# Four graph layers in one kernel: the rows of layer 2's next block are made two to three chunks sooner, and layer 1 gets one more step before its row of scores

## The chip, the cores and the metric

The kernel runs on one core of a Trainium2 chip. A core has a matrix engine (TensorE, PE in the profile, with its weight loads as PEld), a vector engine (VectorE, DVE), an activation engine (ScalarE, ACT), a general engine (GpSimd, POOL) and an engine that here only issues transfers (SyncE, SP). The metric is device time in microseconds; the figure of a kernel is the median of its runs.

## The reference

The input is a matrix x of 2708 nodes by 512 features, and an adjacency matrix adj of 2708 x 2708 with ones on its diagonal. Four layers follow each other. Each adds a graph operation to x and normalises the rows:

```python
x = layernorm(x + L0(x, adj))   # attention with 8 heads, masked by adj
x = layernorm(x + L1(x, adj))   # D^-1/2 (adj+I) D^-1/2 ((x W1' + b1) W2' + b2)
x = layernorm(x + L2(x, adj))   # additive attention, below
x = layernorm(x + L3(x, adj))   # relu(D^-1/2 (adj+I) D^-1/2 x W)
```

The change is in layers 1 and 2. Layer 2 is

```python
s1 = (h @ W[:512]) @ a_w ;  s2 = (h @ W[512:]) @ a_w
e = s1[:, None] + s2[None, :] + a_b
e = where(e >= 0, e, 0.2 * e) ;  e = where(adj > 0, e, -9e15)
out = softmax(e, axis=1) @ (h @ fc_w + fc_b)
```

So a score needs one number of the query node (s1) and one of the key node (s2). The softmax needs, for each query, the largest score, and because the leaky step only rises, that is found from the largest s2 among the query's neighbours.

## The kernel before

The 2708 nodes are 22 chunks of 128 rows, the last of 20. They are also 6 blocks (NB) of 512 columns, the last of 148, which is 4 chunks a block and 2 in the last. All data is fp32.

**Layer 1** (graph1 L828, finish1 L857). For each block b of output columns graph1 goes over the 22 chunks m: it loads a piece of the transposed adjacency (adjT, load_adjT L607, on SP's queue, eight buffers), multiplies it with H[m] into two PSUM banks, and adds up column sums on DVE (L848). The rest of block b is done by finish1(b), a generator that is advanced while the *next* block is being multiplied, once after every chunk m with m % 4 == 3: at each step one chunk is mapped, added and normalised, and its score s2 is computed as a **column** (score L703, L707: one number per partition, in s2c). When all chunks of the block are through, one further step turns the columns into a **row** that is the same on all 128 partitions (spread_block L645, spread L635: for every chunk one matmul of the broadcast column with the identity, two PE instructions each, into a PSUM tile psds, then one ACT copy L643 into s2b). What is left of the generator is run off after the block, before the next generator is made. Block 5's finish1 is advanced in the first part of layer 2, after every odd chunk.

The row s2b is read by top2 (L696, L698): for 128 query rows it takes the largest of s2 over their neighbours in a stretch of adj. For block 0 this is done during layer 1 in three pieces (piece L898, top0 L908), the second piece of each of its four chunks at chunks 0 to 3 of block 5; that piece ends at column 2048, so it reads the rows of blocks 0 to 3. Its loads have two buffers, and they stand in SP's queue among the adjT loads.

**Layer 2** (graph2 L1007, weigh L787, softmax2 L773, product L726). For a block b of 512 queries and each chunk m of 128 keys, ACT masks the adjT piece (L694) and makes the leaky scores from the query row s1b and the key column s2c (Prelu, L781), DVE subtracts the mask (L782) and the row of maxima mxb (L783), ACT takes Exp (L784), PE multiplies the result pt with x into four PSUM banks (L731, 8 PE instructions a chunk), and POOL adds up the sums (L795). There are six pt buffers, eight adjT buffers, six accumulator banks and two further PSUM banks (ps_m) for everything else.

Block 0 is done in two parts: chunks 0 to 15 with preliminary maxima while the last nodes are still being normalised, and chunks 16 to 21 afterwards with the final ones.

The two rows that a block needs, s1b and mxb, come from row_lines (L770): again columns into rows by spread, 8 PE instructions and one ACT copy each. The columns for block b + 1 come from class Maxima (L936), whose steps are taken while block b is multiplied: one step begins two loads of adj, each of the other eight masks half a stretch of adj, takes its largest s2, and every second one ends with row_max (L755), which writes a column of mxc. In blocks 1 and later the steps are taken after even chunks, so the ninth comes after chunk 16. For block 1 six of them are taken in the first part of block 0 and three after chunks 16, 17 and 18. The call of row_lines stands in the loop at L1072, after chunk 20.

The finished block is mapped with fc_w by finish2 (L1025), also a generator: ACT copies four accumulators (L1037), and after chunks 3, 7, 11 and 15 of the next block one chunk each is multiplied (L743, tile pf in ps_m), added by DVE (L1048) and normalised.

**What sets the order.** In layer 0 the order on PE, DVE and ACT is written out by hand. From layer 1 on it is made by the framework's planner when the kernel is built: it goes through the instructions by its own estimates of their durations, gives each engine what is ready, earliest in the program first, and fixes one order for each engine. On the chip each engine then keeps to that order. A few instructions (held, for Maxima and its loads) are pinned behind what precedes them in the program on their engine.

Of the kernel before, what the change touches and what calls it, by code (L numbers as in the profile page):

```python
# [22 lines left out]
def kernel(  # L23
# [27 lines left out]
    NC = (N + P - 1) // P  # L51
    NB = (N + BLK - 1) // BLK
    QSCALE = 1.0 / KD**0.5

    def rows(c):
        return c * P, min(P, N - c * P)

    def cols(b):
        return b * BLK, min(BLK, N - b * BLK)

    def chunks_of(b):
        n0, w = cols(b)
        return [n0 // P + i for i in range((w + P - 1) // P)]
# [37 lines left out]
    def layernorm(dst, y, q):  # L101
        st = small.tile([P, 6], F32, tag="lnst", name="lnst")
        nc.vector.bn_stats(st[:q], y)
        mv = small.tile([P, 2], F32, tag="lnmv", name="lnmv")
        nc.vector.bn_aggr(mv[:q], st[:q])
        ve = small.tile([P, 1], F32, tag="lnve", name="lnve")
        nc.vector.tensor_scalar(ve[:q], mv[:q, 1:2], LN_EPS, None, ALU.add)  # L107
        rs = small.tile([P, 1], F32, tag="lnrs", name="lnrs")
        rsqrt(rs[:q], ve[:q], q, 1, "ln")
        nc.vector.tensor_scalar(dst, y, mv[:q, 0:1], rs[:q], ALU.subtract, ALU.mult)  # L110
# [524 lines left out]
    def spread(dst, columns, name):  # L635

        w = sum(q for _, q in columns)
        pd = ps_m.tile([P, BLK], F32, tag="m", name=f"psd{name}")
        o = 0
        for col, q in columns:  # L640
            nc.tensor.matmul(pd[:, o : o + q], col.to_broadcast([q, P]), ident[:q, :q], start=True, stop=True)
            o += q
        nc.scalar.copy(dst, pd[:, :w])  # L643

    def spread_block(dst, cols_of, b, name):  # L645
        spread(dst, [(cols_of[: rows(c)[1], c : c + 1], rows(c)[1]) for c in chunks_of(b)], name)

    def column_sums(sums, b, name):

        w = cols(b)[1]  # L650
        pc = ps_m.tile([P, 4], F32, tag="m", name=f"pcs{name}")
        for i, c in enumerate(chunks_of(b)):
            q = rows(c)[1]
            nc.tensor.matmul(pc[:q, i : i + 1], sums[:, i * P : i * P + q], ones, start=True, stop=True)
        return pc
# [47 lines left out]
    def score(dst, c, of, held=False):  # L703

        q = rows(c)[1]
        pr = io.tile([P, D], F32, tag="y", name=f"pr{of}_{c}")
        tt = nc.vector.tensor_tensor_reduce(  # L707
            out=pr[:q],
            in0=X[c][:q],
            in1=ub[:q, of, :],  # L710
            scale=1.0,
            scalar=0.0,
            op0=ALU.mult,
            op1=ALU.add,
            accum_out=dst[:q, c : c + 1],
        )
        if held:
            tc.keep_in_program_order(tt)
        if of == 0:
            nc.vector.tensor_scalar(dst[:q, c : c + 1], dst[:q, c : c + 1], gab_sb[:q], None, ALU.add)  # L720

    def accs(name):

        return [ps_acc.tile([P, BLK], F32, tag="acc", name=f"acc{name}_{k}") for k in range(KC)]
# [45 lines left out]
    def row_lines(b, maxs, name=""):  # L770
        return row_line(b, s1c, "s1b"), row_line(b, maxs, "mxb")
# [26 lines left out]
    if True:  # L798
# [58 lines left out]
        def finish1(b):  # L857

            n0, w = cols(b)
            yt, sums = done1[b]  # L860
            pc = column_sums(sums, b, f"1_{b}")
            for i, c in enumerate(chunks_of(b)):
                q = rows(c)[1]
                rc = small.tile([P, 1], F32, tag="rc1", name=f"rc1_{c}")
                nc.vector.tensor_tensor(rc[:q], pc[:q, i : i + 1], rdeg[:q, c : c + 1], ALU.mult)
                p2 = ps_m.tile([P, BLK], F32, tag="m", name=f"p2_{c}")
                for hc in range(HC):
                    nc.tensor.matmul(
                        p2[:q, :], yt[:, hc, i * P : i * P + q], w2_sb[:, hc, :], start=(hc == 0), stop=(hc == HC - 1)
                    )  # L870
                y = io.tile([P, D], F32, tag="y", name=f"y1_{c}")
                nc.vector.scalar_tensor_tensor(y[:q], b2_sb[:q], rc[:q], X[c][:q], ALU.mult, ALU.add)
                nc.vector.scalar_tensor_tensor(y[:q], p2[:q, :], rdeg[:q, c : c + 1], y[:q], ALU.mult, ALU.add)
                layernorm(X[c][:q], y[:q], q)
                score(s2c, c, 1)
                yield
            spread_block(s2b[:, n0 : n0 + w], s2c, b, f"s2_{b}")
            yield

# [126 lines left out]
    if True:  # L1006
        def graph2(b):  # L1007
            m0 = CUT // P if b == 0 else 0
            acc = accs(f"2_{b}")
            sums = cap2.tile([P, BLK], F32, tag="cs", name=f"cs2_{b}")  # L1010
            for m in range(m0, NC):
                weigh(b, m, acc, sums, m0)
                yield m
            done2[b] = acc, sums

        def first_part(yt):

            f = io.tile([P, BLK], F32, tag="y", name="f2")
            nc.vector.tensor_tensor(f, lines_a[1], lines[0][1], ALU.subtract)
            nc.scalar.activation(f, f, AF.Exp)  # L1020
            for k in range(KC):
                nc.vector.tensor_tensor(yt[:, k, :], acc_a[k], f, ALU.mult)
            nc.vector.tensor_tensor(sums_a, sums_a, f, ALU.mult)

        def finish2(b):  # L1025
            w = cols(b)[1]
            cs = chunks_of(b)
            acc, sums = done2[b]
            if b == 0:
                yt = yt0  # L1030
                for k in range(KC):
                    nc.vector.tensor_tensor(yt[:, k, :], yt[:, k, :], acc[k], ALU.add)
                nc.vector.tensor_tensor(sums, sums, sums_a, ALU.add)
            else:
                yt = ytp.tile([P, KC, BLK], F32, tag="yt", name=f"yt2_{b}")
                for k in range(KC):
                    nc.scalar.copy(yt[:, k, :w], acc[k][:, :w])  # L1037
            yield
            pc = column_sums(sums, b, f"2_{b}")
            rc = small.tile([P, 4], F32, tag="rc2", name=f"rc2_{b}")  # L1040
            for i, c in enumerate(cs):
                q = rows(c)[1]
                nc.vector.reciprocal(rc[:q, i : i + 1], pc[:q, i : i + 1])
            for i, c in enumerate(cs):
                q = rows(c)[1]
                pz = mapped(yt, i, q, fcw_sb, f"pf{c}")
                y = io.tile([P, D], F32, tag="y", name=f"y2_{c}")
                nc.vector.scalar_tensor_tensor(y[:q], pz[:q, :], rc[:q, i : i + 1], X2[c][:q], ALU.mult, ALU.add)  # L1048
                layernorm(X2[c][:q], y[:q], q)
                yield  # L1050

        def scaled(c):

            q = rows(c)[1]
            nc.vector.tensor_scalar(X[c][:q], X2[c][:q], rdeg[:q, c : c + 1], None, ALU.mult)

        yt0 = ytp.tile([P, KC, BLK], F32, tag="yt", name="yt2_0")
        first_part(yt0)
        fin = iter(())
        for b in range(NB):  # L1060
            if b:
                queue = Maxima(b + 1) if b + 1 < NB else None
            for m in graph2(b):
                if m % 4 == 2 and 0 <= m // 4 < len(chunks_of(b)) and b:
                    c = chunks_of(b)[m // 4]
                    q = rows(c)[1]
                    held(nc.vector.tensor_tensor(X2[c][:q], X[c][:q], fcb_sb[:q], ALU.add))
                if queue and (b == 0 or m % 2 == 0):
                    queue.step()
                if m % 4 == 3:  # L1070
                    next(fin, None)
                if b + 1 < NB and m == NC - 2:  # L1072
                    lines[b + 1] = row_lines(b + 1, mxc)
                if b == NB - 1 and m >= 6:
                    scaled(m - 6)
                if b == 0 and m == NC - 1:
                    for c in chunks_of(0):
                        held(nc.vector.tensor_tensor(X2[c], X[c], fcb_sb, ALU.add))
            for _ in fin:
                pass  # L1080
            fin = finish2(b)
            next(fin)
        for c in range(NC - 6, chunks_of(NB - 1)[0]):
            scaled(c)
# [224 lines left out]
```

## Time and profile before

| | us |
|---|---|
| median of 3 runs (lowest, highest) | 2607.38 (2600.11, 2610.36) |
| the profiled execution | 2611.59 |
| its span, first to last instruction | 2609.8 |
| layer 0 (0 to about 1345 us), PE busy | 1317.5 of 1345 |
| layer 0's end and layer 1 (1345 to 1650), PE busy | 301.1 of 305 |
| first part of layer 2 and its seam (1650 to 1735), PE busy | 74.6 of 85 |
| rest of layer 2 (1735 to 2160), PE busy | 415.3 of 425 |
| layer 3 (2160 to 2610), PE busy | 431.8 of 450 |

How to read it: a row of the waits gives the engine, the line that waited, what released it, the total in us, the number of times, and the longest. A row of the timeline gives start and length in us, the engine, the line, the operation, output and inputs with their shapes, and in brackets how long the engine was idle before it and what ended that. The windows give the busy time of an engine in a stretch with the clock that TensorE was granted (1.00 is full speed). Matmuls in fp32 appear as two PE instructions each.

### The profile page before, as it was taken

Reading aid. Unit: us, or ns where it says so; the run is one execution under the profiler, and the core shown is the slowest. Engines: PE = TensorE matmul, PEld = TensorE weight load, DVE = VectorE, ACT = ScalarE, POOL = GpSimd, SP = SyncE. Lnnn points to the kernel's source line nnn. Section 1 sums busy time; section 2 is a strip of 40 time slices with the busy share of each in tenths; the row PEclk is TensorE's granted clock in tenths of the full one; section 3 lists DMA queues with packets and bytes.
Section 4 is the critical chain, followed back from the end, with each engine's and each line's share of the span. In section 5 each row is a group of like instructions: output and inputs, shape, how many; then the busy total and the mean of one; then the engine's idle time right before and its main releaser. Section 6 shows DMA issues by size and latency. Waiting matters only on the chain.

```text
span 2609.8 us, 42027 instructions
## 1 busy us (share of the span) xinstructions
PE 2540.3 (97%) x15263; PEld 1472.2 (56%) x15263; DVE 1874.5 (72%) x4576; ACT 1212.1 (46%) x2417; POOL 312.0 (12%) x322
## 2 busy tenths in 40 slices
PE   8999999999999999999899999899999999999997
PEld 3445666767676766676546444444444456444465
DVE  2004999999999999998484678978767775453544
ACT  1113778788787787887211001566555640000000
POOL 1110000000000000000220000234333330000000
PEclk9999999999999999999899999989999999999999
DMA  5012888888988888888772544354434213644633
GB/s 199 32 53 58 215 230 217 222 220 209 240 206 210 229 217 216 229 209 184 208 219 76 134 119 139 112 166 135 123 100 129 62 30 108 180 143 141 181 100 107
DMA packets 221445, 411.45 MB, mean 158 GB/s; under 512 B 28711, under 2 KB 48857, under 8 KB 221238
## 3 DMA queue, kind: packets, MB, share of 16 engines
q1 hardware_dynamic: 214998, 392.03, 56.3%
q0 software_dynamic: 6240, 16.73, 1.8%
q8 instruction: 121, 1.98, 0.3%
q14 instruction: 86, 0.70, 0.1%
HBM read 213.57 MB, written 16.72 MB: 88 GB/s over the span
## 4 chain that ended last, share of the span: by engine, by line
PE 77%; issue 9%; DVE 6%; DMA 4%; SPq 2%; ACT 1%; POOL 0%; POOLq 0%; DVEq 0%; ACTq 0%
PE pss L310 15%; PE av L417 14%; PE acc L731 13%; PE acc L837 7%; PE m L1141 6%; PE pf L743 3%; PE psv L250 3%; PE psk L223 3%; PE pst L390 3%; PE psq L223 3%; DMA e<-d 2%; PE po L677 2%; PE ph L823 1%; DVE d L361 1%; SPq L371 1%
## 5 line engine op out<-in xcount | busy, mean ns | idle before, releaser
L332 DVE CUSTOM_DVE_ANT_0 s<-pss,adj 128x512 f32<-128x512 f32 (+1 forms) x1020 | 574.2, 618 | 27.6 <-PE pss L310 26.5
L354 ACT ACTIVATE s<-s,nm 128x1024 f32<-128x1024 f32 (+1 forms) x510 | 527.7, 1037 | 22.9 <-DVE nm L347 22.0
L310 PE MATMUL pss<-KT,qt 64*128 64x512 f32 (+1 forms) x2016 | 463.8, 565 | 7.7 <-DVE mx L332 7.4
L361 DVE STREAM_TRANSPOSE d<-s 128x1024 f32<-128x1024 f32 x340 | 402.4, 1222 | 18.1 <-DMA e<-d 9.0
L731 PE MATMUL acc<-pt,x 128*128 128x512 f32 (+1 forms) x880 | 341.0, 547 | 12.6 <-ACT pt L784 9.7
L417 PEld LDWEIGHTS av<-e,V 128*64 128x64 f32 x5376 | 295.6, 137 | 62.6 <-issue 32.9
L417 PE MATMUL av<-e,V 128*64 128x128 f32 x5376 | 327.4, 275 | 0.0
L310 PEld LDWEIGHTS pss<-KT,qt 64*128 64x128 f32 x2016 | 194.2, 186 | 145.3 <-issue 69.3
L731 PEld LDWEIGHTS acc<-pt,x 128*128 128x128 f32 x880 | 161.1, 196 | 192.1 <-issue 166.0
L837 PE MATMUL acc<-at,h 128*128 128x512 f32 (+1 forms) x504 | 196.8, 543 | 0.0
L795 POOL TENSOR_TENSOR cs<-cs,pt 128x512 f32<-128x512 f32 (+2 forms) x110 | 157.3, 1430 | 202.8 <-ACT pt L784 199.5
L782 DVE TENSOR_TENSOR pt<-pt,at 128x512 f32<-128x512 f32 (+2 forms) x132 | 106.2, 812 | 80.7 <-ACT pt L781 80.5
L1171 ACT ACTIVATE z<-pz,rdeg 128x512 f32<-128x512 f32 (+1 forms) x22 | 15.1, 688 | 312.0 <-PE pz L743 312.0
L438 POOL DMA_DIRECT2D otd<-ot x84 | 45.2, 538 | 959.7 <-ACT ot L437 947.3
L93 ACT ACTIVATE ln_t<-lnve 128x1 f32<-128x1 f32 x88 | 17.7, 201 | 305.7 <-DVE lnve L107 305.7
L391 ACT COPY pt<-pst 128x512 f32<-128x512 f32 x170 | 91.5, 589 | 120.9 <-PE pst L390 120.5
L837 PEld LDWEIGHTS acc<-at,h 128*128 128x128 f32 x504 | 90.2, 190 | 101.4 <-issue 98.7
L417 PEld LDWEIGHTS av<-pt,V 128*64 128x64 f32 x1680 | 90.0, 136 | 64.6 <-ACT adj L185 46.2
L784 ACT ACTIVATE pt<-pt 128x512 f32<-128x512 f32 (+2 forms) x132 | 76.1, 578 | 106.8 <-DVE pt L783 106.6
L848 DVE SCALAR_TENSOR_TENSOR cs<-at,rdeg,cs 128x512 f32<-128x512 f32 (+2 forms) x126 | 86.2, 684 | 43.0 <-DMA at<-in_adjT_dram 41.7
L417 PE MATMUL av<-pt,V 128*64 128x128 f32 x1680 | 110.3, 278 | 1.4 <-ACT ot L437 1.4
L85 DVE COPY KT<-psk 128x512 f32<-128x512 f32 (+1 forms) x12 | 7.5, 629 | 139.5 <-PE psk L223 139.5
(297 smaller groups left out, 3560.4 us busy)
## 6 DMA issues: line engine op xcount, KB each, us to landing
e<-d SPq DMA_DIRECT2D x680, 256.0 KB
at<-in_adjT_dram SPq DMA_DIRECT2D x210, 256.0 KB
a<-in_adj_dram SPq DMA_DIRECT2D x38, 677.0 KB
adj<-in_adj_dram SPq DMA_DIRECT2D x42, 512.0 KB
at_a<-in_adjT_dram SPq DMA_DIRECT2D x40, 256.0 KB
at_c<-in_adjT_dram SPq DMA_DIRECT2D x40, 256.0 KB
at_f<-in_adjT_dram SPq DMA_DIRECT2D x40, 256.0 KB
adj<-in_adj_dram SPq DMA_DIRECT2D x21, 330.0 KB
```

The source lines that it names most:

```text
L223: nc.tensor.matmul(ps[:, :w], w_sb[:, k, p * P : (p + 1) * P], xb[:, k, :w], start=(k == 0), stop=(k == KC - 1),)
L310: nc.tensor.matmul(pss[j][:, :w], qt[h, self.p, :], KT[h, self.p, n0 : n0 + w], start=True, stop=True)
L332: nc.vector.tensor_tensor_reduce(out=s[:, j, h0 : h0 + hw], in0=pss[j][:, :hw], in1=a[:, n0 + h0 : n0 + h0 + hw], scale=1.0, scalar=LOW, o ...
L354: nc.scalar.activation(s, s, AF.Exp, bias=self.nm[j], accum_out=self.sums(j, k))
L361: nc.vector.transpose(self.D[k][:, :, j].rearrange("p i m x -> p m i x"), self.s[k][:, j, : n * P].rearrange("p (m i x) -> p m i x", i=KD4 ...
L391: nc.scalar.copy(sb, pt)
L417: nc.tensor.matmul(self.av[j * KD : (j + 1) * KD, out], V[:, m, h * KD : (h + 1) * KD], weights[j], start=(self.done == 0), stop=(self.don ...
L731: nc.tensor.matmul(acc[k][:, :w], last[0][g : g + mr, :] if m == NC - 1 else values[:mr, k * P : (k + 1) * P], moving[g : g + mr, :w], sta ...
L782: nc.vector.tensor_tensor(pt[:mr, :w], pt[:mr, :w], at[:mr, :w], ALU.subtract)
L795: nc.gpsimd.tensor_tensor(sums[:mr, :w], sums[:mr, :w], pt[:mr, :w], ALU.add)
L837: nc.tensor.matmul(acc[hc][:, :w], lastH[g : g + mr, :] if m == NC - 1 else H[m][:mr, hc * P : (hc + 1) * P], at[g : g + mr, :w], start=(m ...
L1141: nc.tensor.matmul(acc[k][:, : moving.shape[1]], combined[which, m][:, k * P : (k + 1) * P], moving, start=(m == 0), stop=(stop and m == N ...
```

## The change

```diff
         # finish1(b), layer 1
                 layernorm(X[c][:q], y[:q], q)
                 score(s2c, c, 1)
                 yield
+            yield
             spread_block(s2b[:, n0 : n0 + w], s2c, b, f"s2_{b}")
             yield
...
         # the loop over blocks and chunks of layer 2
-                if b + 1 < NB and m == NC - 2:
+                if b + 1 < NB and m == (NC - 4 if b == 0 else NC - 5):
                     lines[b + 1] = row_lines(b + 1, mxc)
```

The first part puts one empty step into finish1 between the last score column and the row. For a block of four chunks the row was written in the program after chunk 19 of the next block; it is now written when the rest of the generator is run off, after that block's chunk 21. For block 5, whose generator is advanced in layer 2, it moves from after chunk 5 to after chunk 7 of the first part.

The second part moves the call of row_lines for the next block: from after chunk 20 to after chunk 18 in block 0, and to after chunk 17 in blocks 1 to 4. These are the first places in the program at which all columns of mxc for the next block have been written.

## The prediction

> **What bounds the kernel.** First the page, for the engine that sets the pace and the chain of work that ended last.
>
> ```profile
> span 2609.8 us, 42027 instructions
> PE 2540.3 (97%) x15263; PEld 1472.2 (56%) x15263; DVE 1874.5 (72%) x4576; ACT 1212.1 (46%) x2417; POOL 312.0 (12%) x322
> PE 77%; issue 9%; DVE 6%; DMA 4%; SPq 2%; ACT 1%; POOL 0%; POOLq 0%; DVEq 0%; ACTq 0%
> ```
>
> TensorE (PE) is the bound: it idles 69.5 us of the span, and only idle time, or time at a low clock, can be won. So I asked next what PE waited for in the two stretches that the change touches: layer 2's blocks (1735 to 2160 us), then the end of layer 1 with the first part of layer 2 (1650 to 1735 us).
>
> ```profile
> PE acc L731 <- ACT pt L784: 9.7, 5, 2.4
> ...
> PE psds L641 <- DVE s2c L707: 5.6, 3, 3.6
> PE acc L731 <- DVE yt L1022: 2.8, 1, 2.8
> ```
>
> The first row is one wait at each of the five block boundaries of layer 2: 2.36, 2.11, 2.11, 2.11 and 1.05 us. The second is the row of s2 of blocks 4 and 5 waiting for a score column: 0.49 and 3.64 us in block 4's row, 1.48 us in block 5's. The third is not touched. The timeline of PE, then of ACT, at the boundary from block 1 to 2 shows how the first wait comes about.
>
> ```profile
> 1823.89 17.33 PE L731 MATMUL acc<-pt,x 128*128 128x512 f32 x40
> 1841.06 1.05 PE L641 MATMUL psds1b<-ident,s1c 128*128 128x128 f32 x8
> 1841.95 1.06 PE L641 MATMUL psdmxb<-ident,mxc 128*128 128x128 f32 x8
> 1842.93 1.14 PE L731 MATMUL acc<-pt,lastX 20*128 20x512 f32 x8
> 1846.18 2.08 PE L731 MATMUL acc<-pt,x 128*128 128x512 f32 x2 [2.11 <-ACT pt L784]
> ```
>
> ```profile
> 1829.53 0.63 ACT L784 ACTIVATE pt<-pt 116x512 f32<-116x512 f32 x1 [0.70 <-DVE pt L783]
> ...
> 1842.15 0.58 ACT L643 COPY s1b<-psds1b 128x512 f32<-128x512 f32 x1 [9.51 <-PE psds1b L641]
> 1842.83 0.72 ACT L781 ACTIVATE pt<-s1b,s2c 128x512 f32<-128x512 f32 x1
> 1843.45 0.57 ACT L643 COPY mxb<-psdmxb 128x512 f32<-128x512 f32 x1
> ...
> 1845.48 0.65 ACT L784 ACTIVATE pt<-pt 128x512 f32<-128x512 f32 x1
> ```
>
> ACT has finished the Exp of block 1's last chunk at 1830.2 and then has nothing to do until PE, twelve microseconds behind, reaches the rows (9.51 us idle). From the end of chunk 20's products (1841.1) the chain is: rows on PE 1.05, copy 0.58, Prelu 0.72, two DVE subtractions 0.69 each, Exp 0.65, with small steps between 5.1 us until 1846.18. PE covers it with the two rows and the short chunk 21, about 3.0 us, and idles the remaining 2.11.
>
> Last, the granted clock. These five windows are where it is halved in this part of the trace.
>
> ```profile
> 1671.94:1675.36 3.42, 3.42 (x7) 0.50 0.14 21
> 1726.56:1733.38 6.82, 6.06 (x7) 0.50 0.50 141
> 1750.45:1757.28 6.83, 6.03 (x7) 0.50 0.41 119
> 1846.02:1849.43 3.41, 3.25 (x4) 0.50 0.42 128
> 2122.50:2125.91 3.41, 3.41 (x16) 0.50 0.31 69
> ```
>
> The columns are window, length, PE busy (instructions), clock, DMA share, GB/s. Each follows one of the PE waits above; the last three follow boundaries 0-1, 1-2 and 4-5.
>
> **Layer 2's rows, part by part.** Nothing is added or removed: 8 PE instructions for each row (0.9 to 1.05 us) and two ACT copies (0.58 and 0.57) move from after chunk 20 to after chunk 17 (after 18 at block 0). They issue no DMA and pass no DMA queue. On PE they pass three chunks of 3.43 us (8 x 0.429, from 17.33/40), 10.3 us (two, 6.9 us, at block 0). That is more than the chain of 5.1 us less the 2.1 us of rows, so the boundary wait should go: **-9.7 us**. What must be there in time:
> - The maxima. Block 1's last column of mxc ends on DVE at 1816.8; the moved row of maxima would start at 1823.89 + 16 x 0.429 + 0.9 = 1831.7. At block 0 the last column ends at 1733.96, and chunk 18 ends about 1739. Covered, with 15 and 5 us to spare.
> - ACT. It is in order, so an Exp behind the copy waits with it. At 1830.2 it is done with the last Exp, so psds1b at 1831.8 finds it idle, and its 9.5 us wait shrinks to about 1.5 us. Eight chunks of the next block are masked by 1832.3, so what follows is Prelu, two subtractions, Exp, limited by the six pt buffers.
> - A PSUM bank. Rows and fc products share two banks, and the second row takes the bank of the fourth fc product, freed by DVE L1048. From that line's four ends (1830.15, 1925.04, 2018.57, 2105.63) against moved starts of 1831.7, 1925.2, 2017.2 and 2108.9, worked out as above, the third is 1.4 us late. Bounds: 0, if DVE, no longer starved at the boundary before, gets there earlier; 1.4 us if not.
> - Accumulator banks. With no gap PE reaches the third bank of the next block 1.7 us after the last one ends; two copies of 0.57 (L1037) must be done. Bounds 0 and 0.5 us a boundary.
> For the last two I take **+1.0 us** in all.
>
> **The clock: row against rule.** The row first: waits of 2.36, 2.11 and 1.05 us were each followed by half clock, two others of 2.11 us were not (1.00 granted). At half clock the 6.03, 3.25 and 3.41 us of PE work cost half of themselves extra: 3.0 + 1.6 + 1.7 = 6.3 us. The Trainium skill, "TensorE: Matmul & The Clock Gate", section "Why this matters for your kernels", puts the danger at PE-idle gaps above about 3 us; by that rule none of these five gaps would cost clock, and the layer-2 gain would be 9.7 - 1.0 = 8.7 us. By the rows it is 9.7 + 6.3 - 1.0 = 15.0 us. I take the rows, since the halved windows begin at the waits: **-6.3 us**. Another execution may fall differently against these windows: 0 to about 9 us.
>
> **Layer 1's extra step.** Four steps of finish1 come at chunks 3, 7, 11 and 15; the row of s2 moves from chunk 19 to the end of the block, past two chunks: at block 3's row x4 at 1.88 us and x4 at 1.13, so 3.0 us. In blocks 0 to 3 no PE wait stands at this row: nothing to win. Block 4's row is already issued piecewise among layer 2's first chunks, later than either place: its 4.1 us wait stays, bounds 0 and -5.8 with the 1.7 us of clock behind it. Block 5's row moves from chunk 5 to chunk 7 of layer 2's first part, 6.9 us of products, past its column at 1687.7: **-1.5 us**. Against that:
> - Block 3's row is read by two L698 at 1627.2, which would start about 1630.2. They free the buffers for two loads that stand in SP's queue at 1628.1, and behind those are layer 1's adjT loads; third and fourth maxima come 3 us later. The cover is that block 5's next adjT slot is not free before about 1630, and that lines[0] is first needed on DVE at 1651.3. If the cover fails, DVE, 38.2 us busy of 40 between 1650 and 1690, passes the delay on: 0 to +3 us; I take +0.5.
> - Block 5's row is read by four L698, and mxc, ready at 1695.6, moves to about 1700, while its PE row stands at 1697.3. If the planner leaves that row after chunk 8, PE waits up to 3 us; if it lets chunk 9 through, about 0.5. I take +1.0.
> Sum of this part: 0.0, between -7 and +5.
>
> **Sum.** -9.7 - 6.3 + 1.0 - 1.5 + 1.5 = -15.0 us on the profiled execution of 2611.6 us (span 2609.8 and 1.8 around it), so 2596.6 there. That execution lies 4.2 us above the median of 2607.4; from the median, **2592.4 us**, 0.58% less. About 0.5%, 13 us, is what a measurement of this kernel can tell from no change, so this forecast sits only 2 us past the line of 2594.4.
>
> **Rivals.**
> 1. The wait goes but the clock pays nothing, because [...] the median runs had few such windows: 2607.4 - 8.7 = 2598.7. For it: the two 2.11 us gaps with full clock. Against: three of five. Chance 0.09, within 0.5%.
> 2. The change doesn't do what it says. The planner puts the copy of s1b on ACT ahead of the Exps of chunks 18 to 21; PE then waits after chunk 17 instead: copy 0.58 + Prelu 0.72 + 1.38 + 0.65 + 1.05 less 2.1 of rows, 2.3 us, what it waits now. About 2607. For it: the order is planned, not measured. Against: ACT's 6.7 to 12.0 us of idle before this copy. Chance 0.08, within.
> 3. Slower, by the bank. If DVE's queue holds L1048 of the fourth fc product behind the next block's first subtraction, the second row waits on PE for copy, Prelu, subtraction and L1048: 0.7 + 0.7 + 1.3 + 0.7 = 3.5 us, with everything on PE behind it. That is long enough for a 6.8 us half-clock window, 3.0 us more. At four boundaries 26 us: 2592.4 + 26 = 2618, and more where a second window falls. It cancels the gain from 15.0/4 = 3.8 us a boundary, clock included. For it: the margins of 1.5, 0.2 and -1.4 us. Against: L1048 is ready two chunks before the row and DVE is 72% busy here. Chance 0.14, of which 0.10 beyond 0.5%.
>
> **How the numbers follow.** My forecast has 0.69: 0.57 beyond the line, 0.12 short of it, because its own range is 2585 to 2599. So faster 0.57; same 0.12 + 0.09 + 0.08 + 0.04 = 0.33; slower 0.10. The range for all goes down to 2583 (all waits of block 4's row gone too: -7.3 more, and 2 of scatter) and up to 2611, where most of rival 3 is left out.
>
> **What would show it.** Right: no PE wait on L784 at the five boundaries, ACT's wait for psds1b under 3 us, the granted clock at 1.00 from 1750 to 2126, a row psdmxb without a PE wait, block 5's row behind chunk 7. Wrong: a new PE wait at psdmxb or after chunk 17 (rivals 3 and 2); half-clock windows elsewhere in layer 2 (rival 1); PE waits between 1626 and 1700 of more than 10 us, against 7.6 now, if the later rows of layer 1 are dearer than I think.

## The result, and the profile after

The time did not change. The median of 22 runs of the changed kernel is 2607.4 us (2603.2 to 2613.8), beside 2607.6 us for 22 runs of the kernel before: a ratio of 1.0004, interval 0.9996 to 1.0013. (Ratios here and below are those on record, over all runs; they lie up to 0.0008 from the quotient of the two medians.) The profiled execution took 2612.9 us. The forecast was 2592.4 us.

In the changed kernel lines behind L877 carry a number one higher than before (L1038 is the copy L1037 of before, L1023 and L1033 are L1022 and L1032). First the page, as for the kernel before.

```profile
span 2611.1 us, 42028 instructions
PE 2544.1 (97%) x15263; PEld 1473.3 (56%) x15263; DVE 1860.2 (71%) x4576; ACT 1215.5 (47%) x2417; POOL 293.2 (11%) x322
PE 71%; DVE 11%; issue 10%; DMA 4%; ACT 2%; SPq 1%; POOL 0%; POOLq 0%; DVEq 0%; ACTq 0%
```

PE is still the bound, and DVE's share of the chain that ended last went up from 6% to 11%. What PE waited for between the start of layer 2 and its end, from the view of the waits (engine, line that waited, what released it, total in us, times, longest):

```profile
PE psdmxb L641 <- DVE mxc L762: 6.6, 1, 6.6
PE acc L731 <- DVE yt L1033: 3.3, 1, 3.3
PE acc L731 <- ACT yt L1038: 3.2, 4, 1.4
PE acc_0a L731 <- ACT pt L784: 2.6, 1, 2.6
PE p L868 <- DVE rc L865: 1.1, 1, 1.1
PE acc_t L731 <- ACT yt L1038: 1.0, 1, 1.0
PE acc L731 <- DVE yt L1023: 0.4, 1, 0.4
```

The five boundary waits on L784, 9.7 us, are gone, and so is the wait for score columns (psds, 5.6 us); L1022's 2.8 us shrank to 0.4. In their place stand two kinds of wait that were not there: 6.6 us for the last maxima, before chunk 9 of layer 2's first part, and 7.5 us for the accumulators to be copied or added away (yt). In all PE waits 18.2 us in this stretch, against 20.0 before.

At the boundary from block 1 to 2 the change did what it says. The timelines of PE and of ACT (start, length, engine, line, operation; in brackets the idle time before it and what ended it):

```profile
1830.58 7.03 PE L731 MATMUL acc<-pt,x 128*128 128x512 f32 x16
1837.44 1.05 PE L641 MATMUL psds1b<-ident,s1c 128*128 128x128 f32 x8
1838.33 1.06 PE L641 MATMUL psdmxb<-ident,mxc 128*128 128x128 f32 x8
1839.23 10.46 PE L731 MATMUL acc<-pt,x 128*128 128x512 f32 x24
```

```profile
1838.54 0.59 ACT L643 COPY s1b<-psds1b 128x512 f32<-128x512 f32 x1 [0.71 <-PE psds1b L641]
1839.21 0.72 ACT L781 ACTIVATE pt<-s1b,s2c 128x512 f32<-128x512 f32 x1
```

The rows stand three chunks (24 PE instructions) ahead of the short last chunk, the second row waits for no bank, and ACT's wait for the row fell from 9.51 to 0.71 us here.

The half-clock windows of the changed kernel in the same part of the trace (window, length, then the busy time of each engine with its instructions, the granted clock, DMA share, GB/s):

```profile
1658.90:1665.70 6.80, 5.83 (x9) 2.73 (x10) 6.80 (x11) 5.24 (x9) 3.06 (x3) 0.50 0.52 167
1706.65:1713.47 6.82, 5.30 (x11) 3.13 (x12) 6.82 (x33) 1.03 (x2) 0.53 (x1) 0.50 0.27 79
1761.30:1764.70 3.40, 3.40 (x5) 1.33 (x4) 3.40 (x9) 1.83 (x3) 0.11 (x1) 0.50 0.57 196
```

They begin at the new waits of 2.6, 6.6 and 3.3 us. In these two executions there are fewer of them than before (17 us in all, against 24). The runs as a whole do not show a gain, and one number per run serves from here on: a stretch at half clock loses half its length, so span x (1 - mean granted clock) is what a run loses by the clock. Before, the mean loss in the four groups of runs made beside the experiments was 21.4, 22.2, 22.1 and 19.7 us, 21.5 over all 134; in the 22 runs of the changed kernel it was 23.3 (standard error 0.8). The change made the clock no better; the 1.8 us by which it looks worse are about two standard errors, and the four groups of the kernel before differ by 2.5 us among themselves. This number is for the whole span: in the profiled executions of all fourteen kernels layer 0, which nothing here touches, lost between about 7 and 14 us, layer 3 about 5 to 8, and layer 2 about 2 to 12.

**Where the 6.6 us come from.** PE, then ACT, then DVE, at chunks 7 to 9 of layer 2's first part:

```profile
1696.33 0.71 PE L641 MATMUL psds<-ident,s2c 128*128 128x128 f32 x4
1696.96 4.56 PE L731 MATMUL acc_0a<-pt,x 128*128 128x512 f32 x10
1708.17 0.80 PE L641 MATMUL psdmxb<-ident,mxc 128*128 128x128 f32 x2 [6.64 <-DVE mxc L762]
```

```profile
1696.72 0.71 ACT L781 ACTIVATE pt<-s1b,s2c 128x512 f32<-128x512 f32 x1
1701.18 1.42 ACT L694 ACTIVATE a<-a,big 128x1354 f32<-128x1354 f32 x1 [3.75 <-DMA a<-in_adj_dram]
...
1703.65 0.26 ACT L643 COPY s2b<-psds 128x148 f32<-128x148 f32 x1
```

```profile
1704.13 1.91 DVE L698 CUSTOM_DVE_ANT_0 ar<-s2b,ar 128x660 f32<-128x660 f32 x1
...
1707.97 0.14 DVE L762 TENSOR_SCALAR mxc<-mx 128x1 f32<-128x1 f32 x1
```

PE's row of block 5 was ready at 1697.0. Its copy on ACT came 6.6 us later, because ahead of it in ACT's queue stood the first mask of Maxima for block 1, and this waited 3.75 us for its load of adj. In the kernel before that copy ran at 1688.2 and the mask at 1697.0: two chunks later put the copy behind the mask. Behind the copy DVE has 4.0 us of maxima (the first column of mxc is ready at 1708.1), then PE may go on.

**Where the 7.5 us come from.** The longest of these waits, 3.3 us, is at the boundary from block 0 to 1, where the accumulators are freed by additions on DVE (L1033) and not by ACT's copies: PE, then DVE.

```profile
1755.67 1.98 PE L731 MATMUL acc<-pt,x 128*128 128x512 f32 x4
1760.93 7.54 PE L731 MATMUL acc<-pt,x 128*128 128x512 f32 x13 [3.28 <-DVE yt L1033]
```

```profile
1757.16 1.64 DVE L783 TENSOR_TENSOR pt<-pt,mxb 128x512 f32<-128x512 f32 x1
1758.72 1.55 DVE L698 CUSTOM_DVE_ANT_0 a<-s2b,a 128x1354 f32<-128x1354 f32 x1
...
1760.20 1.27 DVE L1033 TENSOR_TENSOR yt<-yt,acc 128x512 f32<-128x512 f32 x2
```

Block 0's last product ends at 1755.7, but the first addition starts at 1760.20, behind subtractions for block 1 and a piece of maxima. In the kernel before, the same addition started 0.1 us after that product. The boundary from block 2 to 3 shows it for the pair of ACT's copies: PE, ACT, and one row of DVE.

```profile
1939.85 1.14 PE L731 MATMUL acc<-pt,lastX 20*128 20x512 f32 x8
1940.92 1.98 PE L731 MATMUL acc<-pt,x 128*128 128x512 f32 x4
1944.33 5.85 PE L731 MATMUL acc<-pt,x 128*128 128x512 f32 x13 [1.42 <-ACT yt L1038]
```

```profile
1938.18 1.41 ACT L694 ACTIVATE a<-a,big 128x1354 f32<-128x1354 f32 x1
...
1943.17 0.63 ACT L784 ACTIVATE pt<-pt 128x512 f32<-128x512 f32 x1 [1.75 <-DVE pt L783]
1943.71 1.05 ACT L1038 COPY yt<-acc 128x512 f32<-128x512 f32 x2
```

```profile
1939.62 1.57 DVE L698 CUSTOM_DVE_ANT_0 a<-s2b,a 128x1354 f32<-128x1354 f32 x1 [1.41 <-ACT a L694]
```

Block 2's accumulators are complete at 1941.0. There are six banks, so block 3's chunk 0 fills two, and its third needs a copy. The copy could run at 1941, but in ACT's queue it stands behind an Exp of block 3, and that Exp waits for a subtraction that DVE does only after 1.57 us of maxima (L698) for the block after. With its rows three chunks sooner the next block's work has run so far ahead that the work which frees the banks stands behind it.

This holds for 6.5 of the 7.5 us, at the five boundaries (3.3, 0.2, 1.4, 1.4 and 0.2). The other 1.0 us is at the start of layer 3, where there is no next block of layer 2; it stands in the kernel with the step alone too (1.3 us), so the sooner rows are not needed for it, and its cause stays open.

### The profile page after: what moved, and what is told of

Same layout as the page of the kernel before. It is cut to its first block, busy times and chain, and to the rows that moved or that the text cites. A ratio compares the mean times of both kernels' runs of the same rounds, so it can differ in the third digit from the quotient of the medians.

```text
span 2611.1 us, 42028 instructions
## 1 busy us (share of the span) xinstructions
PE 2544.1 (97%) x15263; PEld 1473.3 (56%) x15263; DVE 1860.2 (71%) x4576; ACT 1215.5 (47%) x2417; POOL 293.2 (11%) x322
## 4 chain that ended last, share of the span: by engine, by line
PE 71%; DVE 11%; issue 10%; DMA 4%; ACT 2%; SPq 1%; POOL 0%; POOLq 0%; DVEq 0%; ACTq 0%
PE pss L310 15%; PE av L417 14%; PE acc L731 8%; PE acc L837 7%; PE m L1142 6%; PE psv L250 3%; PE psk L223 3%; PE psq L223 3%; PE pst L390 3%; PE pf L743 2%; PE po L677 2%; DVE pt L782 2%; DMA e<-d 2%; PE ph L823 1%; DVE d L361 1%
## 5 line engine op out<-in xcount | busy, mean ns | idle before, releaser
L361 DVE STREAM_TRANSPOSE d<-s 128x1024 f32<-128x1024 f32 x340 | 402.4, 1222 | 21.7 <-DMA e<-d 11.8
L417 PEld LDWEIGHTS av<-e,V 128*64 128x64 f32 x5376 | 295.1, 137 | 62.6 <-issue 32.3
L795 POOL TENSOR_TENSOR cs<-cs,pt 128x512 f32<-128x512 f32 (+2 forms) x110 | 135.9, 1236 | 255.2 <-ACT pt L784 249.8
L93 ACT ACTIVATE ln_t<-lnve 128x1 f32<-128x1 f32 x88 | 17.7, 202 | 306.1 <-DVE lnve L107 306.0
L784 ACT ACTIVATE pt<-pt 128x512 f32<-128x512 f32 (+2 forms) x132 | 76.1, 578 | 131.5 <-DVE pt L783 131.1
```

The source lines that it names most:

```text
L361: nc.vector.transpose(self.D[k][:, :, j].rearrange("p i m x -> p m i x"), self.s[k][:, j, : n * P].rearrange("p (m i x) -> p m i x", i=KD4 ...
L417: nc.tensor.matmul(self.av[j * KD : (j + 1) * KD, out], V[:, m, h * KD : (h + 1) * KD], weights[j], start=(self.done == 0), stop=(self.don ...
L795: nc.gpsimd.tensor_tensor(sums[:mr, :w], sums[:mr, :w], pt[:mr, :w], ALU.add)
```

## The experiments

For each kernel: median, ratio to the kernel before with its interval, and what PE's waits show. Each ran beside the kernel before (2607.3, 2606.9, 2606.9 and 2605.1 us in the four groups).

**Each part alone.** First the rows of layer 2 as in the change, without the extra step:

```diff
-                if b + 1 < NB and m == NC - 2:
+                if b + 1 < NB and m == (NC - 4 if b == 0 else NC - 5):
```

> Only the second part of the change: layer 2's rows after chunk 18 in block 0 and after chunk 17 in blocks 1 to 4; layer 1 as before. Theory A (the two parts work against each other: the rows win, the extra step of layer 1 loses as much): the five PE waits on L784 (9.7 us before) are gone, some 3 to 6 us of waits on the accumulators' copies stand in their place, nothing changes before 1720 us, and the time is 4 to 8 us below before (ratio 0.997 to 0.9985). Rival B (the rows win nothing by themselves, because the copies of the accumulators take over the whole wait): within 2 us of before, with copies' waits of about 9 us.

Measured: 2602.8 us, 0.9979 (0.9967 to 0.9991). The waits on L784 are gone; the waits for yt are 1.1, 0.9, 1.4 and 1.4 us at four boundaries. That is the first expectation. This part gains 4.5 us, a third of its forecast.

Then the step of layer 1 alone:

```diff
                 score(s2c, c, 1)
                 yield
+            yield
             spread_block(s2b[:, n0 : n0 + w], s2c, b, f"s2_{b}")
```

> Only the first part: one more step of layer 1 between score columns and row; layer 2's rows as before. Theory A: the second row of maxima of block 0 waits 5 to 7 us on PE for mxc, as in the changed kernel, the five boundary waits on L784 stay, and the time is 2 to 6 us above before (1.001 to 1.0025). Rival B: within 2 us of before, because layer 2's first part waits later anyway (for the vector engine's scaling at L1022) and only swaps one wait for another.

Measured: 2609.4 us, 1.0002 (0.9992 to 1.0012). PE's waits in this kernel begin with:

```profile
PE acc L731 <- ACT pt L784: 9.7, 5, 2.4
PE psdmxb L641 <- DVE mxc L762: 6.5, 1, 6.5
PE acc_0a L731 <- ACT pt L784: 3.2, 1, 3.2
```

So the 6.6 us belong to the step and not to the rows. They take the place of the 5.6 us for columns (gone here too) and of the 2.8 us on L1022 (0.3 here). The interval reaches from 2.1 us below the kernel before to 3.1 above it, so a loss is not shown; what is shown is the swap of waits, the second expectation. By the medians the change is -4.5 and +2.1 us part by part; together -0.2.

**Block 5's share of the step.** Both parts of the change, but no extra step for block 5:

```diff
                 yield
+            if b < NB - 1:
+                yield
             spread_block(s2b[:, n0 : n0 + w], s2c, b, f"s2_{b}")
```

> Both parts, but without the extra step for block 5, whose row of s2 goes back to chunk 5 of layer 2's first part. Theory A with its cause in block 5's late row (its copy stands behind a mask that waits for a transfer): no PE wait of more than 2 us at the row of maxima of block 0, time as with the rows alone, 4 to 8 us below before. If the loss comes from blocks 0 to 4 instead: time as the changed kernel, within 2 us of before.

Measured: 2603.3 us, 0.9982 (0.9974 to 0.9991). That is the first expectation. The wait at psdmxb is gone, and the time is 4 us below the changed kernel: block 5's step is what cancels the gain of the rows. Not all of the 6.6 us come back, for PE now stands 3.7 us at the map of block 5 (L868) and 4.9 us at the seam (yt, L1022 of before).

**Is it the load?** The changed kernel with the two loads for Maxima issued two chunks sooner, ahead of the loads of lastX and s2l on SP:

```diff
-            if m == 8 or m >= 11:
+            if m == 6 or m >= 11:
                 queue.step()
```

> The changed kernel with one edit: the two loads of adj for the next block's first maxima are issued after chunk 6 of the first part in place of chunk 8, so that they stand on SP ahead of the loads of lastX and s2l. Theory (block 5's row is late because its copy stands on ACT behind a mask that waits 3.75 us for that load): the mask's wait for the transfer is gone or under 1 us, PE's wait for mxc before chunk 9 falls from 6.6 to about 3 us, and the time by 3 to 5 us, to 2602 to 2604. Rival (DVE, which has some 6 us of work between the row and the last maximum, is late by itself): the wait stays over 5 us, 2606 to 2608.

Measured: 2598.5 us, 0.9972 (0.9964 to 0.9980). ACT, then PE, of this kernel:

```profile
1694.57 1.41 ACT L694 ACTIVATE a<-a,big 128x1354 f32<-128x1354 f32 x1
...
1699.50 0.26 ACT L643 COPY s2b<-psds 128x148 f32<-128x148 f32 x1
```

```profile
1704.27 0.49 PE L641 MATMUL psdmxb<-ident,mxc 128*128 128x128 f32 x2 [3.01 <-DVE mxc L762]
```

The mask waits for no transfer, and PE's wait fell from 6.64 to 3.01 us, as the theory had it. A wait of 2.4 us for a column of block 4's row, which the changed kernel lacks, came in return. The time fell more than the theory had it, by 8.9 us from the changed kernel: PE's waits are 3.9 us less, and the loss by the clock went from 23.3 to 18.3 us. That the mask waited for its load is shown as the cause of half the wait; the other half, as the timeline reads, is the row's turn on ACT and DVE's maxima.

**When do the rows come too soon?** The kernel before, with its rows after chunk 18, and after chunk 19, in every block:

```diff
-                if b + 1 < NB and m == NC - 2:
+                if b + 1 < NB and m == NC - 4:
```

```diff
-                if b + 1 < NB and m == NC - 2:
+                if b + 1 < NB and m == NC - 3:
```

> Layer 2's rows after chunk 18 in every block, one chunk later than the change in blocks 1 to 4 and the same in block 0; layer 1 as before. Theory (the further ahead ACT and DVE may run, the more of the next block's work stands in their queues in front of the copies that free the accumulators): the PE waits on these copies lie between those of the rows after 17 (1.13 + 0.86 + 1.38 + 1.36 us) and those after 19 (0.35 us in all), 1 to 4 us in sum; time between the two, 6 to 12 us below before (0.9954 to 0.9977). Rival (the gain of the rows after 19 comes from somewhere else than the copies): time as with the rows after 17, or as with the rows after 19, without a change of the copies' waits.

> Layer 2's rows after chunk 19 in every block, between the old place and the new; layer 1 as before. Chain of 5.1 us against 2.1 us of rows, one chunk of 3.4 and the short chunk of 1.1, so the waits on L784 should be gone here too. Theory A with the accumulators' copies late because ACT and DVE are filled with the next block's work before the old one ends: less of it is ahead, so the waits on the copies are smaller than with the rows after 17 and 18 (0 to 3 us in sum), and the time is 7 to 12 us below before. Rival: copies wait as long as with the rows after 17; no better than those.

Measured: after chunk 18, 2603.5 us, 0.9980 (0.9971 to 0.9989), with waits for yt of 1.1, 1.4, 1.4 and 1.4 us, no better than after chunk 17: the expectation of a value between the two places failed, in time and in waits. After chunk 19, 2592.8 us, 0.9946 (0.9932 to 0.9959), with no wait above 0.4 us between blocks (1.2 at the start of layer 3). PE and ACT after chunk 19, at the boundary from block 2 to 3:

```profile
1914.20 3.60 PE L731 MATMUL acc<-pt,x 128*128 128x512 f32 x8
1917.73 1.14 PE L731 MATMUL acc<-pt,lastX 20*128 20x512 f32 x8
1918.80 9.71 PE L731 MATMUL acc<-pt,x 128*128 128x512 f32 x22
```

```profile
1919.22 0.57 ACT L1037 COPY yt<-acc 128x512 f32<-128x512 f32 x1
1919.69 0.63 ACT L784 ACTIVATE pt<-pt 128x512 f32<-128x512 f32 x1
1920.22 1.06 ACT L1037 COPY yt<-acc 128x512 f32<-128x512 f32 x2
1921.16 1.44 ACT L694 ACTIVATE a<-a,big 128x1354 f32<-128x1354 f32 x1
```

One full chunk of cover is enough for the rows, and PE runs on without a gap. The first copies now stand *ahead* of the mask for the maxima (L694 at 1921.16, behind three of them); after chunk 17 that mask ran at 1938.18, 5.5 us before the first copy. So it is not a matter of degree: it turns on which side of the mask and the maxima the copies fall, and one chunk of 3.4 us decides that.

**The copies by order.** If the order is the cause, the rows may stay after chunk 17 when the next block's chunks 2 to 7 are pinned behind the copies (freed[0] is the last instruction of L1037, or L1032, for the block before; the lines that set it are left out):

```diff
-                weigh(b, m, acc, sums, m0)
+                if b and 2 <= m < 8:
+                    with tc.issue_after(freed[0].ins):
+                        weigh(b, m, acc, sums, m0)
+                else:
+                    weigh(b, m, acc, sums, m0)
```

> Layer 2's rows where the change has them (after 18 in block 0, 17 in blocks 1 to 4), layer 1 as before, and an order given to ACT (DVE at the first boundary): chunks 2 to 7 of a block stand behind the copies of the accumulators of the block before. Theory: only the place of the copies in the queue makes PE wait, so the four waits of 4.7 us become less than 1.5 us in sum, no wait on L784 comes back, and the time is 8 to 14 us below before (0.9946 to 0.9969). Rival: the copies aren't the limit, and holding the next block's chunks back makes PE wait for L784 at chunk 2; time no better than the rows alone (0.9979).

Measured: 2609.9 us, 1.0007 (0.9995 to 1.0019). The waits for yt between blocks are gone, so the order of the copies is shown as their cause. But the time is not won, and both expectations missed. PE, then DVE, at the rows before the boundary from block 2 to 3 (L1054 is L1048 of before):

```profile
1911.96 1.05 PE L641 MATMUL psds1b<-ident,s1c 128*128 128x128 f32 x8
1916.39 2.07 PE L641 MATMUL psdmxb<-ident,mxc 128*128 128x128 f32 x8 [3.38 <-DVE y L1054]
```

```profile
1914.99 0.69 DVE L783 TENSOR_TENSOR pt<-pt,mxb 116x512 f32<-116x512 f32 x1
1915.60 0.74 DVE L1054 SCALAR_TENSOR_TENSOR y<-pf,rc,x 128x512 f32<-128x512 f32 x1
```

With its lead taken away DVE reaches the fourth fc product later than the moved row needs its bank: 1.2, 3.4 and 3.3 us at three boundaries. It is the bank of the forecast's rival 3, and near its 3.5 us, but not by its chain: there L1048 was to stand behind the *next* block's first subtraction, and here it stands behind the subtraction for this block's own short last chunk (the row of 116 partitions at 1914.99). That the size agrees is luck. The lead that puts the copies late is what kept the bank free; in these kernels rows after chunk 17 paid for one or the other.

**The changed kernel with its rows after chunk 19**, to see whether the two costs are separate:

```diff
-                if b + 1 < NB and m == (NC - 4 if b == 0 else NC - 5):
+                if b + 1 < NB and m == NC - 3:
```

> The changed kernel with layer 2's rows made after chunk 19 in every block; layer 1's extra step stays, block 5's too. Theory (two separate costs: the copies that free the accumulators, and block 5's row behind a mask on ACT): the waits for yt at the boundaries of layer 2 go as with the rows after 19 alone, the wait of about 6.6 us for psdmxb before chunk 9 of the first part stays. 2607 - 14 + 3 = 2596, between 2593 and 2599. Rival (the step and the rows hurt each other, and the gain of the rows after 19 is gone with the step): 2603 to 2608.

Measured: 2601.5 us, 0.9979 (0.9969 to 0.9989), between the two expectations. The waits for yt went (0.4 us at most, 1.0 at the start of layer 3), the 6.5 us at psdmxb stayed. The waits are the theory's, the time is 5.5 us above its 2596; the clock accounts for most of that: the loss is 22.9 us, against 18.1 with rows after 19 alone.

Then with both repairs:

```diff
-            if m == 8 or m >= 11:
+            if m == 6 or m >= 11:
...
-                if b + 1 < NB and m == (NC - 4 if b == 0 else NC - 5):
+                if b + 1 < NB and m == NC - 3:
```

> The changed kernel with both repairs: layer 2's rows after chunk 19 and the loads after chunk 6 of the first part. Theory (the two costs are separate, so the repairs add up): the yt waits at the boundaries at 0.4 us or less, the wait for mxc before chunk 9 at about 3 us, 2607 - 5.5 - 8.4 = 2593, between 2590 and 2596. Rival (they overlap): no better than the better one alone, 2597 to 2601.

Measured: 2593.3 us, 0.9961 (0.9947 to 0.9976). The waits are as expected (3.6 us at psdmxb, 0.4 between blocks), and the two repairs add up: the costs are separate.

**What of the rest of the first part?** Three kernels tried to win more there, all with rows after chunk 19 and no extra step in layer 1. In the first, block 4's row is made after chunk 4 of the first part, in the second the rows of blocks 4 and 5 are both made after chunk 6 (the spread_block calls of finish1 are left out for these blocks and put into the loop), in the third the loads come after chunk 6:

```diff
+            if m == 4:
+                n0, w = cols(NB - 2)
+                spread_block(s2b[:, n0 : n0 + w], s2c, NB - 2, "s2_late")
```

```diff
+            if m == 6:
+                for c in (NB - 2, NB - 1):
+                    n0, w = cols(c)
+                    spread_block(s2b[:, n0 : n0 + w], s2c, c, f"s2_{c}")
```

```diff
-            if m == 8 or m >= 11:
+            if m == 6 or m >= 11:
```

> Rows after chunk 19 in every block, and the row of s2 of block 4 made after chunk 4 of layer 2's first part instead of piecewise among its first chunks; block 5's row and all else of layer 1 as before. Theory: the 0.49 and 3.65 us waits of that row go, with the half-clock window that follows; 2 to 6 us below the rows after 19 alone, 16 to 20 us below before (0.9923 to 0.9939). Rival: this stretch is bound by DVE (38.2 of 40 us busy before), so PE waits elsewhere in it as long: as the rows after 19 alone, 0.994 to 0.996.

> Layer 2's rows after chunk 19, and the s2 rows of blocks 4 and 5 both made after chunk 6 of the first part, so that PE never stands at a row whose column is missing. Theory (those 7 us of PE waits for psds are idle time that can be filled): they go, no wait of over 1 us takes their place, 2586 to 2590. Rival (DVE sets the pace of this stretch, so a wait taken away there comes back at the next thing that PE needs from DVE): the sum of PE's waits between 1650 and 1735 stays within 2 us, 2591 to 2598.

> The kernel before with layer 2's rows after chunk 19 and the two loads of adj issued after chunk 6 of the first part; no extra step in layer 1. Theory (two separate gains: the rows free the boundaries, the earlier loads free ACT's queue in the first part): PE's wait for the column of block 5, 3.0 us with the rows after 19 alone, does not depend on these loads, but later masks do; 2588 to 2593. Rival (in this order of work ACT's queue isn't held by the load, so the edit moves nothing): as with the rows after 19 alone, 2592 to 2595.

Measured: 2598.0 us, 0.9958 (0.9943 to 0.9973); 2598.5 us, 0.9971 (0.9960 to 0.9982); 2597.7 us, 0.9973 (0.9963 to 0.9982). None is better than the rows after 19 alone. The first comes out as its second expectation; the second just misses both of its own, with 2.7 us more of waits and 0.5 us above the range. In the second PE's waits from the start of the first part to the seam sum to 11.4 us, against 8.7 with rows after 19 alone: the columns' wait came back as one of 5.3 us for block 5's, and 2.6 us at the seam. DVE has 38.7 us of work from 1645 to 1685 (PE 38.9), and 36.0 in the next 40 us, where the 5.3 us wait lies (PE 32.3). That fits a stretch that DVE paces, in which a row moved on PE only moves PE's wait; no run takes work off DVE there to show it. The third missed both of its expectations by 3 to 5 us: without the extra step ACT's queue is not held at that load, so the edit had nothing to win, and what it lost instead (waits 2 us longer in the first part, 2.2 us of them at the seam) is seen but not explained.

**The account.** For each kernel, PE's waits from the start of layer 2 to its end in the profiled execution, the loss by the clock as the mean over its runs (standard errors 0.6 to 1.2), the two changes added up against the kernel before (20.0, and the 21.5 of above, or its own group's for the experiments), and the median's change against that group. A wait of layer 3 that falls at the edge of the stretch in two kernels is left out.

| kernel | PE waits | clock loss | sum of changes | measured |
|---|---|---|---|---|
| changed | 18.2 | 23.3 | 0.0 | -0.2 |
| rows alone | 16.5 | 18.7 | -6.2 | -4.5 |
| step alone | 21.9 | 23.3 | +3.8 | +2.1 |
| no step for block 5 | 17.4 | 21.3 | -2.7 | -4.0 |
| rows after 18 | 15.8 | 19.4 | -7.0 | -3.4 |
| rows after 19 | 10.4 | 18.1 | -12.9 | -14.5 |
| after 17, copies first | 19.3 | 25.0 | +2.1 | +3.0 |
| after 19, block 4's row late | 12.3 | 22.1 | -7.8 | -8.9 |
| after 19, both rows late | 13.1 | 21.5 | -7.5 | -8.5 |
| after 19, loads sooner | 12.3 | 19.2 | -8.2 | -7.4 |
| changed, rows after 19 | 12.6 | 22.9 | -6.6 | -5.5 |
| changed, loads sooner | 14.3 | 18.3 | -9.5 | -8.4 |
| changed, both repairs | 9.8 | 17.7 | -12.2 | -11.8 |

The two columns account for every kernel but one within 2 us, and for that one within 4. This is a check by size: the waits are of one execution, the loss is of the whole span.

**The best version.** Rows after chunk 19 with nothing else changed (0.9946, interval 0.9932 to 0.9959) and the changed kernel with both repairs (0.9961, 0.9947 to 0.9976) beat both the kernel before and the changed one. Both rest on six runs, and their intervals overlap; the first is an edit of one digit.

## Why the prediction was wrong

**Right.** The reading of the boundary: PE's 2.11 us as rows made too late, and the -9.7 us for it. All five waits went, ACT's wait for the row fell below 3 us at four boundaries (at the last it is 4.9), no row of maxima waited on PE for the bank, block 5's row stands behind chunk 7, and its 1.5 us wait went. The bank's 1.4 us of lateness at one boundary did not appear, so its lower bound held. Rival 2 did not happen. Rival 3 did not happen either: its bank was waited for only when the next block's lead was taken away, and by another chain. Rival 1's half came true: the boundary waits went, and over all runs the clock paid nothing. Two slips in the working change nothing: 0.429 us is 17.17/40, not 17.33/40, and rival 3's terms add up to 3.4 us.

**Step "Accumulator banks. [...] Bounds 0 and 0.5 us a boundary."** This failed, as the term that decided layer 2. It took two copies of 0.57 us, ready to run when PE's last product ended, and asked only for their length. The runs showed 3.3 us at the first boundary, where the banks are freed by DVE's additions and not by these copies, about 1.4 at two others and 0.2 at the rest: 6.5 us, and 7.5 with the 1.0 at the start of layer 3, where +1.0 had been taken for this and the bank together. What was left out is their place in the queue. The forecast worked out that ACT was idle after 1830.2 and let the next block's Prelu and Exp start there, and so put in front of the copies just what they would wait behind. It looked for an Exp stuck behind the copy of a row (rival 2), not for a copy stuck behind an Exp.

**Step "Block 5's row [...] If the planner leaves that row after chunk 8, PE waits up to 3 us".** The upper bound was too low: 6.64 us, where +1.0 was taken. The forecast followed the row from PE to DVE's L698, but not through ACT's queue, in which the two chunks carried the copy past a mask whose load was not yet there. It asked which loads on SP the moved row is put behind or ahead of for block 3's row, and not for block 5's.

**Step "I take the rows, [...] -6.3 us" of the clock.** It failed. The half-clock windows of one execution were read as if they were the kernel's. Over 22 runs the changed kernel lost 23.3 us by the clock, 1.8 us more than before. What the five waits of 1.0 to 2.4 us cost in clock, the experiments do not settle. Without them the loss was 2.7 us below that of the kernel before (rows alone), 2.8 (after 18) and 3.3 (after 19), but only 0.1, 0.6 and 0.5 us in the three further kernels with rows after 19 and no step (each figure has a standard error of 1 us or more). The traces say more: these five waits were followed by half clock three times in the kernel before and once in the kernel with the step alone, which has the same five, so they cost about 6.8 us in one execution and 1.7 in the other. So the forecast's 6.3 was the dear one of two cases, and neither was the nothing that the Trainium skill's "TensorE: Matmul & The Clock Gate", "Why this matters for your kernels", would give for gaps that short. The wait of 6.6 us, well above that page's figure of about 3 us, cost clock as the page would have it: with the step the loss is 1.9, 4.6 and 4.8 us higher than without it (on the kernel before, the rows as in the change, the rows after 19), and with the loads mended it is 5.0 and 5.2 us lower again. So the clock of the short waits was overrated, and that of a long new wait was missing from the sum.

**Block 4's row, "its 4.1 us wait stays".** It went: one of the two bounds, but not the one taken. With it went 2.5 us at the seam. These 6.6 us paid for block 5's row, which is why the step by itself is near nothing.

**The sum.** Waits were forecast at -8.7 and came to -1.8: +6.5 for the accumulators (with layer 3's start), +5.6 for block 5's row, -6.6 for block 4's row and the seam, +1.8 for the later start of layer 2 and its first maps, and -0.5 for block 3's row, at which no wait of its own was seen. The clock was forecast at -6.3 and came to +1.8. Together 0.0 in place of -15.0. The forecast's sign of being wrong there, "PE waits between 1626 and 1700 of more than 10 us", was too narrow: the wait that mattered began at 1701.5. Two other signs did show: a new PE wait at psdmxb, though in the first part and not for rival 3's reason, and a half-clock window inside 1750 to 2126.

## What to carry to other kernels

When something is made sooner, everything that it lets start is made sooner too and stands in the in-order queues ahead of whatever frees what the next stage needs: for each buffer or bank, ask where in the queue its release will stand, not how long it takes. So move by the cover that is missing and no more: here the chain of 5.1 us less 2.1 of rows needed 3.0 us of cover; one full chunk and the short last one gave 4.5, and two full chunks were already too many. A gain in clock is not to be read from the windows of one trace: take the mean granted clock of many runs, and the traces of all kernels that share the wait.

## What the runs showed of the hardware

The loss by the clock is not a fixed tax. Between kernels whose PE work is the same it went from 17.7 to 25.0 us. In four kernels one wait of PE was above 5 us (the changed one, the step alone, the changed one with rows after 19, both rows late: 23.3, 23.3, 22.9 and 21.5 us lost), and in the four kernels with the least loss none was above 3.8 us (17.7, 18.1, 18.3 and 18.7). It isn't only the longest wait, though: 25.0 us, the most, was lost with three waits of 3.3 to 3.6 us and others below, and the kernel before, with none above 3.7, lost 21.5.

The fourteen traces together show which waits are followed by half clock. Between 1640 and 2165 us every stretch at half clock begins during a PE wait or within 2 us of its end. Counted over all waits of 0.9 us or more:

| PE wait | waits | with half clock |
|---|---|---|
| 5 us and more | 4 | 4 |
| 3 to 5 us | 19 | 18 |
| 2 to 3 us | 19 | 9 |
| 0.9 to 2 us | 46 | 3 |

The stretches are 3.4 or 6.8 us long, once 10.2 after two waits of 3.6 and 3.4 us close together. So in these traces a wait of 2 to 3 us is a toss-up, and the same 2.11 us wait was followed by half clock in one of six cases. What decides such a case stays open.
